# Writing own-column rows from a resident tile instead of gathering them, and leaving W times a to the general path

## The chip, the cores and the metric

The kernel runs on one core of one Trainium2 chip. The metric is the device time of one execution in microseconds. Each run of the kernel executes the whole program once; three runs of the kernel before gave 234.99 to 235.19 us, median 235.16.

## The reference

A graph attention layer with four heads, followed by a residual sum and a layer norm, all in float32, N = 4096 nodes with D = 512 features:

```python
ht = (h @ W).reshape(N, 4, 512).transpose(1, 0, 2)
src = einsum('hnd,hd->hn', ht, a_src); dst = einsum('hnd,hd->hn', ht, a_dst)
e = leaky_relu(src[:, :, None] + dst[:, None, :], 0.01) + adj[None]
att = softmax(e, axis=-1)
out = layernorm(x + einsum('hij,hjd->hid', att, ht).mean(axis=0))
```

`adj` (4096 x 4096) holds zeros and, at the edges and on the whole diagonal, values drawn uniformly from 0.05 to 1e9. It is added to the scores inside the softmax. Where the largest value of a row exceeds the second by more than the scores can differ, the softmax is one at that column and zero elsewhere, for all heads alike. Then row i of the output is layernorm(x[i] + x[col(i)] @ mean of the heads of W), with col(i) the column of the row's largest value.

## The kernel before

`leading_rows` computes that short form for all rows, and a test proves for each row that it is exact. The test compares the gap between a row's two largest values with a bound on the scores: the largest norm of a row of x times the largest sum of two norms of W times a. `general`, the full computation, stands behind a branch that is taken only where the test fails for some row.

The 4096 rows are cut into 32 blocks of 128. Block ib takes rows p*32 + ib, one for each partition p. For each block:

- `load_adj` loads the adjacency tile adj_t, 128 x 4096, 2 MB, on the SP queue. Six buffers; in iteration t the tile of block t+5 is issued, which waits until VectorE has read the tile of block t-1.
- `segment_maxima` (line 180, VectorE) reduces each row to the maxima of segments of 16 values (32 from block 18 on, 64 for the last four).
- `find_segment` (lines 187, 189, VectorE) finds the largest segment, and `fetch_segment` (lines 196, 200, POOL) fetches that segment of each row from memory by an indirect DMA into the tile lead.
- `find_column` (lines 217, 223, VectorE; 225, POOL) finds the place within the segment, adds the segment's start on POOL, and `gather_rows` (line 211, POOL) fetches row col of x for each of the 128 rows by an indirect DMA into the tile y, 256 KB a block. y has four buffers.
- `turn` (line 238 TensorE, 240 ScalarE) transposes y into yt; `residual` (line 246) puts x's own rows, resident in the tile hold, into the PSUM tile o by a product with the identity; `products` (line 253) adds yt times w_sum, the mean of W's heads.
- `stats` (lines 275, 277, ScalarE) sums o and its squares, `row_norm` (line 260, ScalarE) sums the squares of x's row for the bound, `rstd` (lines 280 to 282, POOL) makes the factor of the layer norm, `finish` (line 286, ScalarE) writes the result into hold, and stores follow after the loop.

hold is one tile for all 32 blocks. Its upper half holds W at first, 16 pieces of 128 x 512; x's blocks from 16 on are loaded over it once W is used.

W times a is computed in iterations 1 to 14, one or two pieces an iteration: `turn_w` transposes a piece (line 359 TensorE, 361 ScalarE), and `head_vector` multiplies it with the transposed a (line 367). `head_norms` makes the norms in iteration 16.

The order on every engine is the order in which the program emits the instructions (`tc.manual_schedule()`); each engine runs its queue in that order. The main loop runs t from 0 to 31 and emits, in this order: the loads of SP; the first half of block t's segment maxima; find_column of block t-2 with its gather; the second half; rstd for a pair of blocks (even t); find_segment of block t with its fetch; the transposes of W; turn, residual and products of block t-3; stats and row_norm of block t-4; the two finishes of the pair. Blocks 24 to 31 leave this pattern: blocks 24 to 27 are put by without the residual, and blocks 28 to 31 are finished after the loop.

Of the kernel before, what the change touches and what calls it, by code (L numbers as in the profile page):

```python
# [26 lines left out]
LAST = 4  # L27


@with_exitstack  # L30
def gat_resnorm_kernel(
    ctx: ExitStack,
    tc: tile.TileContext,
    x: bass.AP,
    adj: bass.AP,
    W: bass.AP,
    a: bass.AP,
    out: bass.AP,
):
# [19 lines left out]
    v = keep.tile([P, KB, 2 * H], F32, name="v")  # L59
    n_bad = keep.tile([1, NB], I32, name="n_bad")  # L60
    any_bad = keep.tile([1, 1], I32, name="any_bad")

    leading_rows(tc, x, adj, W, a, out, ident, v, n_bad, any_bad)

    flag = nc.values_load(any_bad[0:1, 0:1], min_val=0, max_val=N)
    with tc.If(flag > 0, preferred_fallthrough_block=True, label="general"):
        general(tc, x, adj, W, out, ident, v, n_bad)
# [3 lines left out]
def leading_rows(ctx, tc, x, adj, W, a, out, ident, v, n_bad, any_bad):  # L71
# [11 lines left out]
    KB, NB = D // P, N // P  # L83
    AHEAD = 5
# [5 lines left out]
    once = ctx.enter_context(tc.tile_pool(name="once", bufs=1))  # L90
# [3 lines left out]
    LEADS = (8, 8, LAST)  # L94
    small = ctx.enter_context(tc.tile_pool(name="small", bufs=5))
# [6 lines left out]
    x_rows = x.rearrange("(p nb) d -> p nb d", nb=NB)  # L102
    out_rows = out.rearrange("(p nb) d -> p nb d", nb=NB)
# [3 lines left out]
    once.tile([P, 24], F32, name="pad")  # L107
    hold = once.tile([P, NB, D], F32, name="hold")
    w_at = NB - KB * H
    w_sum = once.tile([P, KB, D], F32, name="w_sum")  # L110
    a_rows = once.tile([2 * H, D], F32, name="a_rows")

    once.tile([P, 32], F32, name="pad_end")
# [5 lines left out]
    def load_adj(ib):  # L119
        if 0 <= ib < NB:  # L120
            t = adj_t[ib] = adj_pool.tile([P, N], F32, name="adj_t")
            n = pieces(ib)
            for k in range(n):
                nc.sync.dma_start(t[:, ts(k, N // n)], adj_rows[ib][:, ts(k, N // n)])  # L124

    def load_x(lo, n):
        nc.sync.dma_start(hold[:, ds(lo, n), :], x_rows[:, ds(lo, n), :])
# [19 lines left out]
    for e, lo, hi in spans:  # L147
        nc.gpsimd.iota(
            first[:, lo:hi], pattern=[[N // e, hi - lo]], base=lo * N // e, channel_multiplier=NB * N // e
# [10 lines left out]

# [47 lines left out]

    def gather_rows(ib, col):
        y = y_t[ib] = y_pool.tile([P, D], F32, name="y")  # L210
        nc.gpsimd.indirect_dma_start(  # L211
            out=y, out_offset=None, in_=x,
            in_offset=bass.IndirectOffsetOnAxis(ap=col[:, :1], axis=0),
        )

# [18 lines left out]
    def turn(ib):  # L234
        y = y_t.pop(ib)
# [3 lines left out]
        yt = yt_of[ib] = rows.tile([P, KB, P], F32, name="yt")  # L239
        nc.scalar.copy(yt, tp)  # L240

# [95 lines left out]
    def store(queue, lo, n):  # L337
        queue.dma_start(out_rows[:, ds(lo, n), :], hold[:, ds(lo, n), :])
# [7 lines left out]
    at_d = once.tile([P, KB, 2 * H], F32, name="at_d")  # L346
    vn = once.tile([P, 1], F32, name="vn")
    pv = psum.tile([P, KB, 2 * H], F32, name="pv", bufs=1)

    def turn_a():  # L350
        tp = psum.tile([P, KB, P], F32, name="tp", bufs=2)
        for k in range(KB):
            nc.tensor.transpose(tp[:, k, : 2 * H], a_rows[:, ts(k, P)], ident[: 2 * H, : 2 * H])
        nc.scalar.copy(at_d, tp[:, :, : 2 * H])

    def turn_w(kb, h):
        tp = psum.tile([P, KB, P], F32, name="tp", bufs=2)
        for k in range(KB):
            nc.tensor.transpose(tp[:, k, :], hold[:, w_at + kb * H + h, ts(k, P)], ident)  # L359
        wt = rows.tile([P, KB, P], F32, name="wt")  # L360
        nc.scalar.copy(wt, tp)  # L361
        return wt

    def head_vector(kb, h, wt):

        for k in range(KB):
            nc.tensor.matmul(  # L367
                pv[:, kb, h : 2 * H : H], wt[:, k, :], at_d[:, k, h : 2 * H : H],
                start=(k == 0), stop=(k == KB - 1),
            )  # L370

    def head_norms():
        nc.vector.tensor_copy(v, pv)
        vv = once.tile([P, KB, 2 * H], F32, name="vv")
        nc.vector.tensor_mul(vv, v, v)
        pn = psum.tile([P, KB, 2 * H], F32, name="px", bufs=1)
        nc.tensor.matmul(pn, ones, vv, start=True, stop=True)
        n2 = once.tile([P, 2 * H], F32, name="n2")
        nc.vector.tensor_reduce(n2, pn.rearrange("p k c -> p c k"), axis=AX.X, op=OP.add)
# [47 lines left out]
    x_at = {Q - 1: (Q, 2 * Q), 3 * Q - 1: (3 * Q, Q), 4 * Q - 1: (4 * Q, 2 * Q)}  # L427
    vectors = [(kb, h) for kb in range(KB) for h in range(H)]
    vectors_at = {t: 2 if t < 3 else 1 for t in range(1, 15)}
    COLUMN, PROJECT, STATS, FINISH = 2, 3, 4, 6  # L430

    for t in range(NB):
# [12 lines left out]
        pair = FINISH <= t < BEHIND + FINISH and t % 2 == 0  # L445
# [11 lines left out]
        if t == 0:  # L457
            turn_a()
        turned = [(*vectors[0], turn_w(*vectors.pop(0))) for _ in range(vectors_at.get(t, 0))]
# [97 lines left out]
def general(ctx, tc, x, adj, W, out, ident, v, n_bad):  # L557
# [10 lines left out]
    H = v.shape[2] // 2  # L568
# [9 lines left out]
    with ExitStack() as pre:  # L578
        sd_all = pre.enter_context(tc.tile_pool(name="all", bufs=1)).tile([2 * H, N], F32, name="sd_all")
# [4 lines left out]
        for kb in range(KB):  # L584
            nc.gpsimd.dma_start(w_sb[:, kb, :], w_blocks[:, kb, :])
        for g in range(NCH):
            xT = two.tile([P, KB, C], F32, name="xT")
            for q in range(Q):
                ps = pps.tile([P, KB, P], F32, name="ps_x")
                for kb in range(KB):  # L590
                    nc.tensor.transpose(ps[:, kb, :], x_sb[:, g * Q + q, ds(kb, P, KB)], ident)
# [11 lines left out]
        for g in range(NCH):  # L603
            pt = pps.tile([P, Q, 2 * H], F32, name="ps_s")
            for q in range(Q):
                rows_of = sd_all[:, ds(g * Q + q, P, NB)]
                nc.tensor.transpose(pt[:, q, :], rows_of, ident[: 2 * H, : 2 * H])
            nc.vector.tensor_copy(src[:, ts(g, Q), :], pt[:, :, :H])
# [6 lines left out]
    def block(ib):  # L615
        src_i = stat.tile([P, H], F32, name="src_i", bufs=1)
        nc.vector.tensor_copy(src_i, src[:, ds(ib, 1), :].rearrange("p o h -> p (o h)"))
        held = psum.tile([P, D], F32, name="o_ps", bufs=1)
        adj_t = score.tile([P, N], F32, name="adj_g")
        nc.gpsimd.dma_start(adj_t, adj[ds(ib, P, NB), :])  # L620
# [39 lines left out]
        nc.gpsimd.dma_start(r, x[ds(ib, P, NB), :])  # L660
# [10 lines left out]
        nc.gpsimd.dma_start(out[ds(ib, P, NB), :], r)  # L671

    with tc.For_i(0, NB, 1) as ib:
        of_block = stat.tile([1, 1], I32, name="of_block", bufs=1)
        nc.vector.tensor_copy(of_block, n_bad[0:1, ds(ib, 1)])
        here = nc.values_load(of_block[0:1, 0:1], min_val=0, max_val=P)
        with tc.If(here > 0):
            block(ib)
# [28 lines left out]
```

## Time and profile before

| what | value |
|---|---|
| median of three runs | 235.16 us |
| span of the profiled execution, first to last instruction | 233.4 us |
| VectorE busy | 191.3 us (82%) |
| TensorE matmuls busy | 199.9 us (86%) |
| ScalarE busy | 111.8 us (48%) |
| POOL busy | 100.7 us (43%) |
| bytes moved by DMA | 97.12 MB |
| mean granted TensorE clock | 0.965 |

The times of the trace count from the start of the span. The runs' times hold in addition what lies before the first and after the last instruction; the median is 1.8 us above the span. The profiled execution has no other time of its own than its span. In a line of a group or timeline, the text behind the length is engine, line, operation, the tile written and the tiles read, and in brackets the idle time before it and what ended it.

### The profile page before, as it was taken

What the parts mean: (1) busy time and instruction counts of PE and PEld (TensorE: products, weight loads), DVE (VectorE), ACT (ScalarE), POOL (GpSimd) and SP (SyncE); (2) the same over time, 40 slices, a digit from 0 to 9 for tenths busy, and PEclk for the clock granted to TensorE, in tenths of its full rate; (3) what the DMA queues carried; (4) which work ended last, traced back from release to release, by engine and by line L of the source; (5) the groups of instructions that cost most, each with busy time, mean ns of one, the idle gap of its engine ahead of it and who ended that gap; (6) DMA issues with size and microseconds to landing.
All of it is one profiled execution on the core that took longest, in us unless ns stands there. A gap on an engine that the chain in (4) does not pass through costs nothing.

```text
span 233.4 us, 2484 instructions
## 1 busy us (share of the span) xinstructions
PE 199.9 (86%) x683; PEld 105.3 (45%) x683; DVE 191.3 (82%) x300; ACT 111.8 (48%) x267; POOL 100.7 (43%) x215
## 2 busy tenths in 40 slices
PE   0069995999999999999999779879998977999980
PEld 0034644646565555665645244334443433444460
DVE  0548299689929999999788995999999999998881
ACT  2001223014474757575767455545664644188561
POOL 2020234414524464644543452647464564548300
PEclk9999999579999999999999979999999999999997
DMA  6999999999999999999999999999999999999995
GB/s 237 423 432 428 428 438 426 415 439 436 422 421 437 423 431 425 431 419 428 430 430 428 432 423 432 423 430 421 426 433 420 426 423 426 412 424 420 421 414 213
DMA packets 12257, 97.12 MB, mean 416 GB/s; under 512 B 1992, under 2 KB 2440, under 8 KB 6480
## 3 DMA queue, kind: packets, MB, share of 16 engines
q1 hardware_dynamic: 8640, 88.08, 89.1%
q0 software_dynamic: 3584, 8.84, 9.6%
q8 instruction: 6, 0.10, 0.2%
q14 instruction: 11, 0.09, 0.1%
q10 hardware_dynamic: 16, 0.02, 0.0%
HBM read 88.54 MB, written 8.39 MB: 415 GB/s over the span
## 4 chain that ended last, share of the span: by engine, by line
DMA 64%; DVE 21%; PE 11%; SPq 1%; issue 1%; ACT 0%; DVEq 0%
DMA adj_t<-in_adj_dram 53%; DVE seg L180 17%; DMA hold<-in_x_dram 11%; PE o L253 6%; PE o L295 2%; DVE at L189 1%; PE tp L238 1%; DVE top L187 1%; PE o L246 1%; DVE within L223 1%; SPq L130 1%; PE o L291 0%; SPq L124 0%; DVE inner L217 0%; ACT hold L335 0%
## 5 line engine op out<-in xcount | busy, mean ns | idle before, releaser
L180 DVE TENSOR_REDUCE seg<-adj_t 128x128 f32<-128x2048 f32 (+3 forms) x66 | 145.5, 2208 | 28.5 <-DMA adj_t<-in_adj_dram 28.2
L253 PE MATMUL o<-w_sum,yt 128*128 128x512 f32 x248 | 117.6, 616 | 0.7 <-ACT yt L240 0.7
L253 PEld LDWEIGHTS o<-w_sum,yt 128*128 128x128 f32 x248 | 45.6, 196 | 55.2 <-issue 43.9
L240 ACT COPY yt<-tp 128x512 f32<-128x512 f32 x32 | 18.8, 588 | 43.9 <-PE tp L238 43.8
L200 POOL DMA_INDIRECT lead<-in_adj_dram,row x32 | 32.3, 1008 | 14.6 <-POOL row L196 14.6
L211 POOL DMA_INDIRECT y<-in_x_dram,col x32 | 30.9, 964 | 15.4 <-POOL col L225 15.1
L238 PE MATMUL tp<-ident,y 128*128 128x128 f32 x128 | 22.1, 296 | 10.2 <-DMA y<-in_x_dram,col 10.1
L246 PE MATMUL o<-hold,ident 128*128 128x512 f32 x52 | 28.5, 634 | 1.7 <-DMA hold<-in_x_dram 1.7
L343 PE MATMUL o<-hold,ident 128*128 128x512 f32 x32 | 17.3, 696 | 13.6 <-DMA hold<-in_L_gnn_W_dram 13.6
L238 PEld LDWEIGHTS tp<-ident,y 128*128 128x128 f32 x128 | 18.5, 209 | 22.8 <-issue 20.5
L361 ACT COPY wt<-tp 128x512 f32<-128x512 f32 x16 | 9.2, 587 | 38.2 <-PE tp L359 38.2
L196 POOL TENSOR_TENSOR row<-at,first 128x1 uint32<-128x1 uint32 x32 | 6.1, 190 | 43.6 <-DVE at L189 43.6
L367 PEld LDWEIGHTS pv<-at_d,wt 128*128 128x128 f32 x128 | 17.2, 200 | 7.4 <-ACT wt L361 3.7
L260 ACT ACTIVATE sq<-hold 128x512 f32<-128x512 f32 x32 | 19.8, 620 | 0.0
L225 POOL TENSOR_TENSOR col<-start,within 128x1 uint32<-128x1 uint32 x31 | 5.9, 190 | 32.2 <-DVE within L223 32.2
L286 ACT ACTIVATE hold<-o,nm,sd 128x512 f32<-128x512 f32 x24 | 17.2, 771 | 0.0
L277 ACT ACTIVATE sq<-o,nm 128x512 f32<-128x512 f32 x24 | 16.5, 687 | 0.8
L343 PEld LDWEIGHTS o<-hold,ident 128*128 128x128 f32 x32 | 6.9, 225 | 21.5 <-issue 21.5
L367 PE MATMUL pv<-at_d,wt 128*128 128x2 f32 x128 | 16.0, 249 | 0.6 <-ACT wt L361 0.6
L344 ACT ACTIVATE w_sum<-o 128x512 f32<-128x512 f32 x4 | 2.4, 598 | 27.5 <-PE o L343 27.5
L275 ACT ACTIVATE sq<-o 128x512 f32<-128x512 f32 x24 | 14.5, 606 | 0.0
L187 DVE MAX8 top<-seg 128x8 f32<-128x256 f32 (+2 forms) x32 | 11.6, 362 | 1.1
(86 smaller groups left out, 140.0 us busy)
## 6 DMA issues: line engine op xcount, KB each, us to landing
adj_t<-in_adj_dram SPq DMA_DIRECT2D x28, 2048.0 KB, 30.8
adj_t<-in_adj_dram SPq DMA_DIRECT2D x6, 1024.0 KB, 28.1
hold<-in_L_gnn_W_dram SPq DMA_DIRECT2D x2, 2048.0 KB, 16.4
hold<-in_x_dram SPq DMA_DIRECT2D x2, 2048.0 KB, 37.6
out_dram<-hold SPq DMA_DIRECT2D x4, 1024.0 KB, 16.1
out_dram<-hold SPq DMA_DIRECT2D x7, 512.0 KB, 14.4
hold<-in_x_dram SPq DMA_DIRECT2D x3, 1024.0 KB
adj_t<-in_adj_dram SPq DMA_DIRECT2D x4, 512.0 KB, 19.8
```

The source lines that it names most:

```text
L180: nc.vector.tensor_reduce(seg_of[ib][:, ts(k, N // e // n)], adj_t[ib][:, ts(k, N // n)].rearrange("p (s e) -> p s e", e=e), axis=AX.X, op ...
L200: nc.gpsimd.indirect_dma_start(out=lead, out_offset=None, in_=adj_segs[e], in_offset=bass.IndirectOffsetOnAxis(ap=row[:, :1], axis=0),)
L211: nc.gpsimd.indirect_dma_start(out=y, out_offset=None, in_=x, in_offset=bass.IndirectOffsetOnAxis(ap=col[:, :1], axis=0),)
L238: nc.tensor.transpose(tp[:, kb, :], y[:, ds(kb, P, KB)], ident)
L240: nc.scalar.copy(yt, tp)
L246: nc.tensor.matmul(o_ps[ib], ident, hold[:, ib, :], start=start, stop=False)
L253: nc.tensor.matmul(o_ps[ib], yt_of[ib][:, kb, :], w_sum[:, kb, :], start=(start and kb == 0), stop=(kb == KB - 1),)
L260: nc.scalar.activation(sq, hold[:, ib, :], AF.Square, accum_out=xx[:, ib : ib + 1])
L277: nc.scalar.activation(sq, o, AF.Square, bias=nm[:, i], accum_out=sd[:, i])
L286: nc.scalar.activation(hold[:, ib, :], o_ps.pop(ib), AF.Identity, bias=nm[:, i], scale=sd[:, i])
L343: nc.tensor.matmul(o, ident, hold[:, w_at + kb * H + h, :], start=(h == 0), stop=(h == H - 1))
L367: nc.tensor.matmul(pv[:, kb, h : 2 * H : H], wt[:, k, :], at_d[:, k, h : 2 * H : H], start=(k == 0), stop=(k == KB - 1),)
```

## The change

Five things are done together.

- In blocks 4 to 23, POOL compares each row's column with the row's own number. ScalarE writes y from hold, x's own rows, scaled by the comparison (one or zero). POOL adds 8192 to the index where the column is the row's own, which puts it beyond the bound of 4095, and the gather skips such rows. The gather writes the other rows of y over the zeros, so it follows ScalarE's write.
- The x loads of blocks 4 to 23 are issued two iterations earlier, since hold is now read one iteration earlier; x's block 0 is loaded by itself.
- The blocks are cut differently: block 0 is rows 0 to 127, and block ib from 1 on takes rows 128 + p*31 + ib - 1.
- The test's bound uses the Frobenius norm of W's heads times the norm of a instead of the norm of W times a. 16 square sums of W's pieces (iterations 3 to 14) and one of a replace the transposes and products; W times a is computed in the general path alone.
- finish runs seven instead of six iterations behind, in odd iterations; PSUM's o has five buffers instead of four, in the place of the tile pv.

```diff
+SKIP = 8192
+OWN = range(4, 24)
...
-    psum = ctx.enter_context(tc.tile_pool(name="psum", bufs=4, space=bass.MemoryType.PSUM))
-    adj_rows = adj.rearrange("(p nb) m -> nb p m", nb=NB)
+    psum = ctx.enter_context(tc.tile_pool(name="psum", bufs=5, space=bass.MemoryType.PSUM))
+    adj_rows = adj[P:, :].rearrange("(p nb) m -> nb p m", nb=RB)
...
     def load_x(lo, n):
-        nc.sync.dma_start(hold[:, ds(lo, n), :], x_rows[:, ds(lo, n), :])
+        if lo == 0:
+            nc.sync.dma_start(hold[:, 0, :], x[:P, :])
+            lo, n = 1, n - 1
+        if n:
+            nc.sync.dma_start(hold[:, ds(lo, n), :], x_rows[:, ds(lo - 1, n), :])
...
+    load_x(0, 1)
     for ib in range(KB // 2 + 1, AHEAD):
         load_adj(ib)
-    load_x(0, Q)
+    load_x(1, Q - 1)
...
+    numbers = once.tile([P, NB], I32, name="numbers")
+    nc.gpsimd.iota(numbers, pattern=[[1, NB]], base=P - 1, channel_multiplier=RB)
+    own = once.tile([P, NB], F32, name="own")
+    nc.gpsimd.tensor_copy(own, numbers)
...
+    def skipped(ib, col):
+        away = None
+        if ib in OWN:
+            y = y_t[ib] = y_pool.tile([P, D], F32, name="y")
+            same = small.tile([P, 1], F32, name="same")
+            nc.gpsimd.tensor_scalar(same, col, own[:, ib : ib + 1], None, op0=OP.is_equal)
+            nc.scalar.activation(y, hold[:, ib, :], AF.Copy, scale=same)
+            away = small.tile([P, 1], U32, name="away")
+            nc.gpsimd.tensor_scalar(away, same, float(SKIP), None, op0=OP.mult)
+        return away
+
     def gather_rows(ib, col):
-        y = y_t[ib] = y_pool.tile([P, D], F32, name="y")
+        if ib not in OWN:
+            y = y_t[ib] = y_pool.tile([P, D], F32, name="y")
+            nc.gpsimd.indirect_dma_start(
+                out=y, out_offset=None, in_=x,
+                in_offset=bass.IndirectOffsetOnAxis(ap=col[:, :1], axis=0),
+            )
+            return
+        there = small.tile([P, 1], U32, name="there")
+        nc.gpsimd.tensor_tensor(there, col, skipped(ib, col), op=OP.add)
         nc.gpsimd.indirect_dma_start(
-            out=y, out_offset=None, in_=x,
-            in_offset=bass.IndirectOffsetOnAxis(ap=col[:, :1], axis=0),
+            out=y_t[ib], out_offset=None, in_=x,
+            in_offset=bass.IndirectOffsetOnAxis(ap=there[:, :1], axis=0),
+            bounds_check=N - 1, oob_is_err=False,
         )
...
+    def square_sum_of_w(k):
+        sq = rows.tile([P, D], F32, name="sq")
+        nc.scalar.activation(sq, hold[:, w_at + k, :], AF.Square, accum_out=ww[:, k : k + 1])
...
-    x_at = {Q - 1: (Q, 2 * Q), 3 * Q - 1: (3 * Q, Q), 4 * Q - 1: (4 * Q, 2 * Q)}
-    vectors = [(kb, h) for kb in range(KB) for h in range(H)]
-    vectors_at = {t: 2 if t < 3 else 1 for t in range(1, 15)}
-    COLUMN, PROJECT, STATS, FINISH = 2, 3, 4, 6
+    x_at = {1: (Q, 2 * Q), 3 * Q - 3: (3 * Q, Q), 4 * Q - 3: (4 * Q, 2 * Q)}
+    squares = list(range(KB * H))
+    squares_at = {t: 2 if t < 7 else 1 for t in range(3, 15)}
+    COLUMN, PROJECT, STATS, FINISH = 2, 3, 4, 7
...
-        for some in turned:
-            head_vector(*some)
-        if ib >= 0:
             products(ib, 0, KB if ib < BEHIND else KB - 1)
+        for _ in range(squares_at.get(t, 0)):
+            square_sum_of_w(squares.pop(0))
```

More of the change, by code (lines that the diff above doesn't have):

```diff
@@ L364, in head_vector @@
[L364 to L370, printed above, removed]
-    def head_norms():
[L373 to L377, printed above, removed]
+    ww = once.tile([P, KB * H], F32, name="ww")
@@ L457, in leading_rows @@
         if t == 0:
-            turn_a()
-        turned = [(*vectors[0], turn_w(*vectors.pop(0))) for _ in range(vectors_at.get(t, 0))]
+            square_sums_of_a()
         if t == 16:
@@ L556, in general @@
 @with_exitstack
-def general(ctx, tc, x, adj, W, out, ident, v, n_bad):
+def general(ctx, tc, x, adj, W, a, out, ident, n_bad):
     nc = tc.nc
@@ L602, in general @@
                 nc.vector.tensor_copy(dst_b[:, h, ts(g, C)], pb)
[L603 to L608, printed above, removed]
+        for ib in range(NB):
+            pt = pps.tile([P, 2 * H], F32, name="ps_s")
+            rows_of = sd_all[:, ds(P + ib - 1, P, RB)] if ib else sd_all[:, :P]
+            nc.tensor.transpose(pt, rows_of, ident[: 2 * H, : 2 * H])
+            nc.vector.tensor_copy(src[:, ib, :], pt[:, :H])
     score = ctx.enter_context(tc.tile_pool(name="score", bufs=1))
```

124 lines of the change are left out of this document (80 added, 44 removed).

## The prediction

> **What bounds the kernel now.** I read the page's header and queues first, then the busy time in stretches, then the waits.
>
> ```profile
> span 233.4 us, 2484 instructions
> DMA  6999999999999999999999999999999999999995
> GB/s 237 423 432 428 428 438 426 415 439 436 422 421 437 423 431 425 431 419 428 430 430 428 432 423 432 423 430 421 426 433 420 426 423 426 412 424 420 421 414 213
> DMA packets 12257, 97.12 MB, mean 416 GB/s; under 512 B 1992, under 2 KB 2440, under 8 KB 6480
> q1 hardware_dynamic: 8640, 88.08, 89.1%
> q0 software_dynamic: 3584, 8.84, 9.6%
> ```
> ```profile
> 53.30:114.90 61.60, 61.60 (x263) 36.95 (x263) 55.45 (x81) 36.47 (x91) 31.14 (x66) 1.00 1.01 427
> 114.90:176.20 61.30, 54.69 (x150) 24.61 (x148) 54.64 (x85) 35.70 (x86) 30.77 (x64) 0.97 1.01 429
> ```
> ```profile
> DVE seg L180 <- DMA adj_t<-in_adj_dram: 28.2, 11, 8.7
> ```
>
> The 16 DMA engines are full from the second slice to the last but one. Between 53.3 and 176.2 us (the columns behind the length are PE, PEld, DVE, ACT, POOL, clock, DMA share, GB/s) the DMA share is 1.01 at 427 to 429 GB/s; VectorE is busy 55.45 of 61.60 us, ScalarE 36.47. VectorE waits for adjacency tiles, 28.2 us in all. So the transfers set the pace, VectorE stands close behind, and ScalarE, POOL and TensorE have room **as throughput**. The change must be judged by latency too, so next come the landings and one block's period.
>
> ```profile
> adj_t<-in_adj_dram SPq DMA_DIRECT2D x28, 2048.0 KB, 30.8
> lead<-in_adj_dram,row POOLq DMA_INDIRECT x32, 6.1
> y<-in_x_dram,col POOLq DMA_INDIRECT x32, 7.8
> DMA to landing us min/median/max: 6.2/7.8/9.5
> ```
> ```profile
> 53.31 2.27 DVE L180 TENSOR_REDUCE seg<-adj_t 128x128 f32<-128x2048 f32 x1
> ...
> 80.49 2.27 DVE L180 TENSOR_REDUCE seg<-adj_t 128x128 f32<-128x2048 f32 x1
> ...
> 86.15 2.27 DVE L180 TENSOR_REDUCE seg<-adj_t 128x128 f32<-128x2048 f32 x1
> ...
> 142.66 2.29 DVE L180 TENSOR_REDUCE seg<-adj_t 128x64 f32<-128x2048 f32 x1 [2.37 <-DMA adj_t<-in_adj_dram]
> 144.86 0.18 DVE L217 MAX8 inner<-lead 128x8 f32<-128x32 f32 x1
> ...
> 176.25 2.29 DVE L180 TENSOR_REDUCE seg<-adj_t 128x64 f32<-128x2048 f32 x1
> ```
>
> The fourth line is the spread of the row gathers of line 211. Iterations 6, 10, 11, 20 and 26 of the main loop start on VectorE at 53.31, 80.49, 86.15, 142.66 and 176.25. Undisturbed, VectorE needs 86.15 - 80.49 = 5.66 us a block. Iterations 6 to 25, in which the changed blocks 4 to 23 get their rows, take 176.25 - 53.31 = 122.9 us, or 6.15 us each, two x loads among them. An adjacency tile lands 30.8 us after its issue: the SP queue holds some five blocks of work, so VectorE may fall many us behind before the DMA engines run dry.
>
> **What the change removes.** Counted on the reference's own inputs, 205 of the 2560 rows of blocks 4 to 23 have their largest adjacency value on the diagonal. Their 205 x 2 KB = 0.42 MB are 1.0 us at 416 GB/s, if a skipped descriptor costs nothing; 0 if it costs what a fetched one does. The second part takes work off TensorE:
>
> ```profile
> L359 PE MATMUL tp<-ident,hold 128*128 128x128 f32 x64 | 9.3, 273 | 0.0
> L367 PE MATMUL pv<-at_d,wt 128*128 128x2 f32 x128 | 16.0, 249 | 0.6 <-ACT wt L361 0.6
> L361 ACT COPY wt<-tp 128x512 f32<-128x512 f32 x16 | 9.2, 587 | 38.2 <-PE tp L359 38.2
> ```
>
> That is 9.3 + 16.0 = 25 us of TensorE in iterations 1 to 14. On ScalarE 16 copies of 0.59 become 17 square sums of the kind of line 260 (below): 0.61 start to start, so nothing is saved there. TensorE does not set the pace, so the 25 us are worth nothing directly. In return the bound becomes looser; on the inputs the smallest gap between a row's two largest values is 10880, against a bound that rises from about 180 to about 1670, so the general path stays unused.
>
> **What it adds on POOL and ScalarE.** Per block there are three POOL instructions (compare, multiply, add) ahead of the gather, and one ScalarE copy that writes the gather's destination y; so the gather must wait for that copy. These rows of iterations 20 and 21 price it:
>
> ```profile
> 146.02 0.97 POOL L211 DMA_INDIRECT y<-in_x_dram,col  x1 [0.54 <-POOL col L225]
> 147.06 0.19 POOL L280 TENSOR_SCALAR sd<-sd 128x2 f32<-128x2 f32 x1
> 147.34 0.72 POOL L281 TENSOR_TENSOR sd<-sd,power 128x2 f32<-128x2 f32 x1
> 147.79 0.72 PE L238 MATMUL tp<-ident,y 128*128 128x128 f32 x4 [0.99 <-DMA y<-in_x_dram,col]
> 148.29 0.19 POOL L196 TENSOR_TENSOR row<-at,first 128x1 uint32<-128x1 uint32 x1
> 148.55 0.59 ACT L240 COPY yt<-tp 128x512 f32<-128x512 f32 x1 [3.49 <-PE tp L238]
> 148.98 1.07 POOL L200 DMA_INDIRECT lead<-in_adj_dram,row  x1 [0.50 <-POOL row L196]
> 149.03 0.60 ACT L275 ACTIVATE sq<-o 128x512 f32<-128x512 f32 x1
> 149.76 0.69 ACT L277 ACTIVATE sq<-o,nm 128x512 f32<-128x512 f32 x1
> 150.44 0.62 ACT L260 ACTIVATE sq<-hold 128x512 f32<-128x512 f32 x1
> 151.05 1.44 ACT L286 ACTIVATE hold<-o,nm,sd 128x512 f32<-128x512 f32 x2
> ...
> 154.62 0.72 PE L238 MATMUL tp<-ident,y 128*128 128x128 f32 x4 [1.73 <-DMA y<-in_x_dram,col]
> ```
>
> A small POOL operation that uses the one before starts 147.34 - 147.06 = 0.28 us after it: three are 0.8 us a block. POOL is busy 31 of 61 us, so as throughput that is covered by its idle time; without the cover it would be 20 x 0.8 = 16 us.
>
> The copy itself is unpriced. The nearest rows, one 128x512 pass, run from 0.59 (L240) to 0.72 (half of the L286 pair); I take 0.62, the row that reads the same tile (L260). **What matters is its place.** In iteration t it is emitted for block t-2 ahead of that iteration's own ScalarE work, so it stands behind all of iteration t-1's: the copy of block t-4's transposed rows (L240), squares, stats (L275, L277), row norm (L260) and, in odd t-1, the pair of finishes (L286). But L240 for block t-4 needs the rows of block t-4's gather. So the gather of block b can't start before the gather of b-2 has landed and been turned. Before, no such tie existed: the gather waited only for POOL's column.
>
> For even b the tie costs, from one gather's start to that of two blocks on: landing 7.8; from TensorE's transposes to the end of the finishes 151.05 + 1.44 - 147.79 = 4.70; the new copy 0.62; **13.1 us**. Where a square sum stands between (iterations 7, 9, 11, 13) it is 0.61 more, by the start-to-start of L260 to L286: 13.7. VectorE does two blocks in 11.3. The finishes move by one iteration (7 instead of 6 behind), which only chooses which parity has them.
>
> **The rule that speaks on this price.** The Trainium skill, page "DMA: Bandwidth & Descriptors", section "Anatomy of one DMA — SWDGE (gpsimd) path", fits such a transfer by 2.0 us and its bytes at 436 GB/s; 256 KB would take an estimated 2.6 us. By that the tie would be 2.6 + 4.70 + 0.62 = 7.9 us and hidden. The trace's 7.8 us, with full queues, decides.
>
> **How it adds up.** The x load of blocks 4 to 11 now goes ahead of adjacency tile 6 instead of tile 8: 2.1 MB at 427 GB/s, so iteration 6 starts 4.9 us later, at 58.2; tile 8 comes as before. Its gather started 146.02 - 142.66 = 3.36 after its iteration; with 0.8 for POOL, block 4's starts at 62.4. Nine steps lead to block 22's: 4 x 13.7 + 5 x 13.1 = 120.3, so 182.7. The next victim is VectorE: POOL fetches block 24's segment (row, lead) behind the gather it waits in: 0.97 + 0.19 + 0.51 + 6.1 = 7.8, so it lands at 190.5. VectorE needs it 144.86 - 142.66 = 2.2 us into iteration 26, which thus starts at 188.3 in place of 176.25: **12.0 us late**. That it is late by less than the sum of the steps' excess is because a gather may trail its column by some 5 us before a segment comes late.
>
> From block 24 on nothing is coupled, and VectorE, full there, can't catch up. Something comes back in the tail, since loads and most stores are done by then:
>
> ```profile
> 202.84 1.22 DVE L180 TENSOR_REDUCE seg<-adj_t 128x16 f32<-128x1024 f32 x1 [0.16 <-DMA adj_t<-in_adj_dram]
> 204.23 0.09 DVE L223 MATCH_VALUE_LOAD within<-top,lead 128x8 f32 x1 [0.17 <-DMA lead<-in_adj_dram,row]
> ...
> 207.19 1.22 DVE L180 TENSOR_REDUCE seg<-adj_t 128x16 f32<-128x1024 f32 x1 [0.23 <-DMA adj_t<-in_adj_dram]
> ```
> ```profile
> 214.56 0.96 POOL L211 DMA_INDIRECT y<-in_x_dram,col  x1 [0.30 <-issue]
> ...
> 221.63 0.72 PE L238 MATMUL tp<-ident,y 128*128 128x128 f32 x4
> ```
> ```profile
> out_dram<-hold SPq DMA_DIRECT2D x2, 256.0 KB, 4.3
> ```
>
> The waits of the last block, 0.16 + 0.17 + 0.23 = 0.6, go. The last gather takes 221.63 - 214.56 = 7.1 until TensorE has it; on emptier queues between 7.1 and the 4.3 of a store of the same size, and the last store gains something as well. I take 3.4 in all for both (bounds 0 and 4). Sum: 12.0 - 0.6 - 3.4 = +8.0 on the span of 233.4, 241.4. The runs' median of 235.16 lies 1.8 above that span, so the forecast is **243.2 us**. The 1.0 us of saved bytes is not in it: in this case the engines wait.
>
> Everything else I cost at nothing. Four short POOL operations at the start are covered: POOL idles there until the first segment is found. The early x load of block 0 (0.26 MB, 0.6 us) delays tile 3, for which VectorE is late anyway. The norms in iteration 16 wait for one product of TensorE, now later with the rest: 0 to 2 us, inside the same lag.
>
> Its own range comes from the landing: nine steps at 7.0 instead of 7.8 take 7.2 off, at 8.5 add 6.3; with the tail's bounds 237 to 250.
>
> **The rivals.**
> 1. *The tie is hidden and the bytes count*: 235.2 - 1.0 = **234.2**. It decides where 13.1 falls to 11.3, so a landing near 6.0. For it: the lowest row gather is 6.2, VectorE is 5.66 against a DMA pace of 6.15, and the TensorE work that goes away stood in front of the transposes. Against: the median is 7.8, and it is contention with queues that stay full.
> 2. *The tie costs just its slack*: at landings near 6.3 VectorE comes a few tenths late and the 1.0 us pays for it: **235.2**.
> 3. *Faster loads*: adjacency rows of one tile lie 31 instead of 32 rows of 16 KB apart. If everything ran at the best slice's 439 GB/s, 149 us of full stages at 427 would shrink by 2.7%, 4 us, and with rival 1 the time is **230**. Against: 427 is within 3% of the best slice already, and transfers don't matter while the tie holds. The same skill page, section "Latency and other measured facts", reports 207 GB/s at a pitch of 512 KiB against 214 padded, per direction; that is 3.4%, which no run here shows.
> 4. *A skipped descriptor is fetched all the same*: rival 1 ends at **235.2**; the forecast does not change.
>
> **Chances.** The forecast 0.74 (slower); rival 1 0.15 and rival 3 0.04 (faster, 0.19); rivals 2 and 4 0.07 (same). About 0.2%, 0.5 us, is what a measurement of this kernel can tell from no change. The forecast's own range of 237 to 250 holds too little alone, so the range reaches to rival 1: 233.8 to 250.
>
> **What would show it.** Right: POOL's row gather waits for ScalarE's new copy in most of blocks 4 to 23; gathers of even blocks start 13 to 14 us apart; VectorE waits for lead at the maxima of line 217 by 10 us or more in all, and for adjacency tiles hardly at all after iteration 12; the DMA share falls in the last fifth. The skipping shows as q0's bytes falling by 0.4 MB. Wrong: a DMA share still at 1.0 throughout, VectorE's waits still for adj_t, landings near 6 us; then the time is rival 1's.

## The result, and the profile after

The changed kernel takes **256.34 us** (median of 4 runs, 254.92 to 257.19) against 235.18 us (4 runs, 234.99 to 235.29) for the kernel before: a ratio of 1.0895 with a 95% interval of 1.0861 to 1.0929. Medians and ratios use the runs within 1.5% of a kernel's fastest; one run of experiment 3, at 259.75 us, lies beyond. The profiled execution took 256.06 us, 254.5 of them in the span: 21.1 us more span than before, where +8.0 was forecast. The sign was right; the time lies 13 us above the forecast and 6 above the range.

The page's header and queues of the changed kernel:

```profile
span 254.5 us, 2248 instructions
DMA  7999999999999999999999999989999999983134
GB/s 248 421 440 426 426 431 425 432 433 421 437 421 439 421 420 434 434 426 431 431 431 426 430 432 417 404 344 396 376 373 396 386 381 418 424 296 89 43 144 194
q0 software_dynamic: 3584, 8.42, 8.8%
```

Its DMA view (KB of one issue, median us from issue to landing):

```profile
adj_t<-in_adj_dram SPq DMA_DIRECT2D x28, 2048.0 KB, 23.7
lead<-in_adj_dram,row POOLq DMA_INDIRECT x32, 6.4
y<-in_x_dram,there POOLq DMA_INDIRECT x20, 8.3
```

The skipping works: q0 moved 8.42 MB instead of 8.84, the 0.42 MB that were counted. But from slice 25 to 35 the rate is 344 to 424 GB/s, and in the last four slices 43 to 194, because the loads have run out while the rest of the kernel is still behind. The time from an adjacency tile's issue on the SP queue to its landing fell from 30.8 to 23.7 us in the median: VectorE frees buffers so late that the queue drains.

The busy time in stretches (length, then PE, PEld, DVE, ACT and POOL busy, clock, DMA share, GB/s):

```profile
53.30:114.90 61.60, 42.00 (x105) 18.89 (x103) 46.93 (x65) 34.24 (x87) 29.77 (x72) 0.92 1.01 428
114.90:176.20 61.30, 46.39 (x122) 21.41 (x122) 45.77 (x74) 34.11 (x80) 32.84 (x82) 0.92 0.99 416
176.20:202.80 26.60, 21.55 (x58) 9.57 (x58) 22.27 (x32) 16.32 (x40) 16.97 (x42) 0.96 0.97 383
202.80:254.50 51.70, 45.03 (x140) 22.62 (x138) 43.43 (x90) 30.68 (x74) 24.08 (x43) 0.96 0.66 251
```

Between 53.3 and 176.2 us TensorE, VectorE and ScalarE are all *less* busy than before: VectorE has 46.93 and 45.77 us where it had 55.45 and 54.64, ScalarE 34.24 and 34.11 where it had 36.47 and 35.70 (TensorE has also lost the work on W times a). Nothing became a throughput bound. Something waits; the waits say what (us in total, times, longest):

```profile
POOL y L245 <- ACT y L230: 29.8, 16, 4.3
DVE seg L194 <- DMA adj_t<-in_adj_dram: 24.2, 5, 8.9
DVE inner L251 <- DMA lead<-in_adj_dram,row: 23.4, 13, 4.2
POOL y L245 <- PE px L403: 3.7, 1, 3.7
DVE w L406 <- PE px L404: 1.9, 1, 1.9
```

POOL's gather (L245) waits for ScalarE's copy (L230) in most of the twenty blocks, and VectorE waits 23.4 us for lead, where it hardly waited before. The wait put down to TensorE's px is a false name: px had nothing to do with that gather, which started at 139.47, 0.80 us after the end of ScalarE's copy (137.96 + 0.71 in the timeline); the two ended close together. So it is with the three gathers whose waits the view puts down to other work: each of the twenty starts 0.77 to 0.80 us after the end of its own copy.

One turn of the loop, from the gather of block 8 to that of block 10, in the chain of waits (start, us, what; "issue" is time without a wait that the profile shows); the first line is block 4's gather:

```profile
62.53 8.79 DMA y<-in_x_dram,there
...
93.77 8.17 DMA y<-in_x_dram,there
101.94 0.14 issue
102.07 1.11 PE tp L271 x4
103.21 0.59 ACT yt L273
103.80 0.62 ACT sq L392 x2
104.42 0.59 ACT sq L312 x2
105.03 0.03 ACT sq L314
105.06 0.55 issue
105.61 0.19 ACT sq L314
105.80 0.61 ACT sq L297 x2
106.41 1.34 ACT hold L323 x2
107.75 0.62 ACT y L230
108.37 0.03 POOLq L245
108.40 0.56 issue
108.98 0.16 issue
109.14 8.39 DMA y<-in_x_dram,there
```

This is the tie of the prediction, link by link: landing, transposes, ScalarE's queue in its order (transposed rows, W's square sum, stats, row norm, the two finishes), the copy, the next gather. It takes 15.37 us for two blocks, and VectorE undisturbed needs 11.3. From block 17 on the chain goes by the odd blocks (gathers at 173.18, 185.87 and 198.04), which have the same tie without the finishes.

### The profile page after: what moved, and what is told of

Same layout as the page of the kernel before. It is cut to its first block, busy times and chain, and to the rows that moved or that the text cites. A ratio compares the mean times of both kernels' runs of the same rounds, so it can differ in the third digit from the quotient of the medians.

```text
span 254.5 us, 2248 instructions
## 1 busy us (share of the span) xinstructions
PE 186.0 (73%) x489; PEld 86.3 (34%) x489; DVE 191.5 (75%) x301; ACT 126.8 (50%) x304; POOL 117.4 (46%) x278
## 3 DMA queue, kind: packets, MB, share of 16 engines
q0 software_dynamic: 3584, 8.42, 8.8%
HBM read 88.54 MB, written 8.39 MB: 381 GB/s over the span
## 4 chain that ended last, share of the span: by engine, by line
DMA 51%; PE 20%; ACT 12%; issue 7%; POOL 4%; DVE 3%; SPq 0%; POOLq 0%
DMA y<-in_x_dram,there 26%; DMA adj_t<-in_adj_dram 20%; PE o L290 12%; PE tp L271 4%; DMA y<-in_x_dram,col 3%; DVE seg L194 3%; ACT hold L323 3%; ACT y L230 2%; DMA lead<-in_adj_dram,row 2%; PE o L283 2%; ACT sq L297 2%; ACT sq L312 2%; ACT yt L273 2%; PE o L332 1%; ACT sq L392 1%
## 5 line engine op out<-in xcount | busy, mean ns | idle before, releaser
L290 PE MATMUL o<-w_sum,yt 128*128 128x512 f32 x248 | 119.5, 624 | 3.4 <-ACT yt L273 3.4
L290 PEld LDWEIGHTS o<-w_sum,yt 128*128 128x128 f32 x248 | 48.0, 203 | 69.5 <-issue 47.8
L273 ACT COPY yt<-tp 128x512 f32<-128x512 f32 x32 | 18.7, 584 | 84.1 <-PE tp L271 83.9
L271 PE MATMUL tp<-ident,y 128*128 128x128 f32 x128 | 23.9, 314 | 45.6 <-DMA y<-in_x_dram,there 34.9
L245 POOL DMA_INDIRECT y<-in_x_dram,there x20 | 22.1, 1105 | 43.2 <-ACT y L230 29.8
L271 PEld LDWEIGHTS tp<-ident,y 128*128 128x128 f32 x128 | 19.5, 209 | 65.5 <-issue 56.1
L214 POOL DMA_INDIRECT lead<-in_adj_dram,row x32 | 32.2, 1008 | 11.6 <-POOL row L210 11.6
L283 PE MATMUL o<-hold,ident 128*128 128x512 f32 x52 | 32.4, 713 | 0.0
L383 PE MATMUL o<-hold,ident 128*128 128x512 f32 x32 | 16.9, 695 | 13.8 <-DMA hold<-in_L_gnn_W_dram 13.8
L251 DVE MAX8 inner<-lead 128x8 f32<-128x16 f32 (+2 forms) x32 | 5.2, 182 | 23.4 <-DMA lead<-in_adj_dram,row 23.4
L230 ACT ACTIVATE y<-hold,same 128x512 f32<-128x512 f32 x20 | 14.3, 717 | 8.6 <-POOL same L229 8.6
L238 POOL DMA_INDIRECT y<-in_x_dram,col x12 | 11.6, 964 | 5.2 <-POOL col L259 4.0
L201 DVE MAX8 top<-seg 128x8 f32<-128x256 f32 (+2 forms) x32 | 11.6, 361 | 1.1
## 6 DMA issues: line engine op xcount, KB each, us to landing
adj_t<-in_adj_dram SPq DMA_DIRECT2D x28, 2048.0 KB, 23.7
```

Of the source, the lines that this page charges most:

```text
L214: nc.gpsimd.indirect_dma_start(out=lead, out_offset=None, in_=adj_segs[e], in_offset=bass.IndirectOffsetOnAxis(ap=row[:, :1], axis=0),)
L230: nc.scalar.activation(y, hold[:, ib, :], AF.Copy, scale=same)
L245: nc.gpsimd.indirect_dma_start(out=y_t[ib], out_offset=None, in_=x, in_offset=bass.IndirectOffsetOnAxis(ap=there[:, :1], axis=0), bounds_c ...
L271: nc.tensor.transpose(tp[:, kb, :], y[:, ds(kb, P, KB)], ident)
L283: nc.tensor.matmul(o_ps[ib], ident, hold[:, ib, :], start=start, stop=False)
L290: nc.tensor.matmul(o_ps[ib], yt_of[ib][:, kb, :], w_sum[:, kb, :], start=(start and kb == 0), stop=(kb == KB - 1),)
```

## The experiments

The edits of 1 to 7 are made to the changed kernel, the later ones to the kernel that each names. Ratios are to the kernel before, with 95% intervals.

**1. The new parts without own-column rows.** No block writes its own rows; the early x loads, W's square sums and the new cut of the blocks stay.

```diff
-OWN = range(4, 24)
+OWN = range(0)
```

> All of the change but the own-column part: no block is compared, copied or skipped; the new cut of the rows, the early x loads, the square sums and the later finishes stay. Theory (the tie between the row gathers of blocks b-2 and b through ScalarE's queue makes the loss): 234.5 to 236, all 21 us come back. Rival (the other parts of the change, above all the cut of the rows and the slower clock of a less busy TensorE, make a good part of it): above 240.

Measured: 235.92 us (235.82 to 236.31), ratio 1.0037 [1.0022, 1.0051]. All but 0.9 of the 21 us comes from blocks 4 to 23's own-column rows. The other parts together bring no gain, so the 25 us of TensorE work that went away bought nothing that shows, as the prediction said.

**2. The copy left out.** The gather waits for nothing of ScalarE. The kernel leaves the own rows unwritten, so its output differs.

```diff
-            nc.scalar.activation(y, hold[:, ib, :], AF.Copy, scale=same)
```

> ScalarE's copy into y is left out, so own rows of y hold what an earlier block left there; the three POOL operations and the skipping gather stay. Theory (tie): 233.8 to 235, the skipped 0.42 MB give about 1 us. Rival (POOL: three operations, and a checked gather of 1.105 us in place of 0.964, 20 times): stays above 245, since nothing of POOL's work is taken away. Rival (skipping itself slows the gather's landing): stays above 245.

Measured: 237.65 us (237.18 to 238.47), ratio 1.011 [1.0081, 1.0138]. One instruction of 0.72 us a block accounts for 18.7 of the 21 us. But the time lies 2.7 us above the expected range and 1.7 above experiment 1; the waits show where.

```profile
DVE inner L250 <- DMA lead<-in_adj_dram,row: 6.8, 11, 1.3
```

**3. Skipping left out.** Own rows are copied and then fetched all the same.

```diff
-SKIP = 8192
+SKIP = 0
```

> 0 in place of 8192 is added to the index, so every row is fetched, also the own ones; copy, comparison and bounds check stay. Theory (tie): 255 to 258, as the change; the bytes return and cost nothing, because the DMA engines are not what is waited for. Rival (skipping slows the landing): back to about 235. Rival (the bytes count even here): 1 us above the change.

Measured: 256.95 us (three runs, 255.68 to 257.08), ratio 1.0906 [1.087, 1.0943]. Against 1.0895 [1.0861, 1.0929] no difference can be told. The intervals reach some 0.8 us to each side, so the 1 us of the second rival isn't excluded; the first, that skipping slows the landing, is.

**4. The copy moved, not removed.** An unconditional copy of x's own rows into y, emitted at the top of an iteration for the block that is gathered in the next one.

```diff
+    def prefill(ib):
+        if ib in OWN:
+            y = y_t[ib] = y_pool.tile([P, D], F32, name="y")
+            nc.scalar.copy(y, hold[:, ib, :])
...
-            nc.scalar.activation(y, hold[:, ib, :], AF.Copy, scale=same)
...
+        prefill(t - 1)
         middle = 1 if t == NB - 1 else 2
```

> The copy into y is made of all rows, without the factor, and one iteration earlier in ScalarE's queue, since the gather overwrites all rows but the own ones; everything else as in the change, and the output is the same. The gather of block b then stands behind that of b-3, not b-2: about 15.2 us over three blocks, 5.1 a block, below VectorE's 5.66. Theory (tie): 234 to 236. Rival (POOL's operations): above 245. Rival (any write of ScalarE ahead of the gather costs, by the 0.77 us that POOL needs after it): about 240 or more.

Measured: 238.11 us (237.8 to 238.9), ratio 1.0137 [1.0114, 1.016]. ScalarE is busy 124.2 us against 126.8 in the changed kernel, and 18.2 us are gone. So what costs is the copy's **place** in ScalarE's queue, not the work that it adds to ScalarE. The time is 2.1 us above the expected range and 2.2 above experiment 1, much as in experiment 2, with VectorE waiting 6.9 us for lead.

**5. Own rows in the first half alone.**

```diff
-OWN = range(4, 24)
+OWN = range(4, 14)
```

> The own-column part for blocks 4 to 13 alone. Theory (tie): up to iteration 16 as in the change, where VectorE is 11.2 us behind the kernel without the part (127.6 against 116.4); from there it runs at its own 5.66 to 5.4 us a block and doesn't wait for the x loads of blocks 16 to 31, which gives some 5 back: 240 to 243. Rival (a loss in proportion to the blocks, 10 of 20): 246 or more.

Measured: 248.53 us (247.81 to 249.5), ratio 1.0569 [1.0533, 1.0605]. My expectation was 5.5 us or more too low; the rival's 246 or more came, though not in proportion to the blocks. VectorE's timeline at iterations 16 and 17 (start, us, instruction, in brackets the idle time before it):

```profile
127.44 2.27 DVE L194 TENSOR_REDUCE seg<-adj_t 128x128 f32<-128x2048 f32 x1
...
140.24 0.17 DVE L406 TENSOR_REDUCE w<-px 128x4 f32<-128x16 f32 x1 [2.72 <-PE px L404]
...
141.22 2.27 DVE L194 TENSOR_REDUCE seg<-adj_t 128x128 f32<-128x2048 f32 x1
...
216.61 1.20 DVE L194 TENSOR_REDUCE seg<-adj_t 128x16 f32<-128x1024 f32 x1
```

I had read the lag off at iteration 16's start, 127.44 - 115.8 = 11.6 us. The last tied gather and the norms then fall into iteration 16 itself, and iteration 17 starts 141.22 - 123.75 = 17.5 us late. From there VectorE caught up to 216.61 - 202.84 = 13.8 us at iteration 31: some 4 us in 14 iterations, because tiles were waiting for it. So the first ten blocks cost 14.0 us of span (247.4) and the last ten 7.1.

**6. The copy twice.**

```diff
             nc.scalar.activation(y, hold[:, ib, :], AF.Copy, scale=same)
+            nc.scalar.activation(y, hold[:, ib, :], AF.Copy, scale=same)
```

> ScalarE writes y twice, with the same values. Theory (tie): each of the nine steps from block 4's gather to block 22's grows by the copy's 0.62 to 0.72 us, 5.6 to 6.5 in all: 261 to 263. Rival (ScalarE has idle time, busy 127 of 254 us, so a copy more is free; the loss comes from POOL or from the landing alone): 256 to 257.

Measured: 262.63 us (262.03 to 263.34), ratio 1.1181 [1.1152, 1.1209], 6.3 us above the changed kernel. Nine steps of 0.62 to 0.72 are 5.6 to 6.5, as expected: what stands in the loop is paid once per step of two blocks, not once per block (twenty copies would be 12 to 14 us).

**7. No copy and no skipping.** Experiments 2 and 3 together.

> No copy into y, and 0 in place of 8192 added to the index: what stays of the own-column part is POOL's three operations and the bounds check. Theory (what was left over without the copy, 237.65 against 235.92, is POOL's longer queue, which fetches the segments late): 237.3 to 239, the skipped bytes being worth 0 to 1 us. Rival (the leftover comes from the skipping itself): 236.

Measured: 239.35 us (237.67 to 239.96), ratio 1.0166 [1.0121, 1.0212]. The leftover is not caused by the skipping. Against experiment 2 (1.011 [1.0081, 1.0138]) the intervals overlap: the bytes are worth between nothing and some 2 us once the tie is gone, which stays open.

**8. Less POOL work ahead of the segment fetch.** Experiment 4, with compare and multiply in one instruction, and the layer norm's factors (rstd) moved behind the fetch.

```diff
-            same = small.tile([P, 1], F32, name="same")
-            nc.gpsimd.tensor_scalar(same, col, own[:, ib : ib + 1], None, op0=OP.is_equal)
             away = small.tile([P, 1], U32, name="away")
-            nc.gpsimd.tensor_scalar(away, same, float(SKIP), None, op0=OP.mult)
+            nc.gpsimd.tensor_scalar(
+                away, col, own[:, ib : ib + 1], float(SKIP), op0=OP.is_equal, op1=OP.mult
+            )
...
-        if pair:
-            rstd(slice(t - FINISH, t - FINISH + 2))
...
         find_segment(t)
+        if pair:
+            rstd(slice(t - FINISH, t - FINISH + 2))
```

> The early copy of all rows, comparison and multiplication in one POOL operation (two on the way to the gather in place of three), and the three POOL operations of the layer norm's factor behind the segment's fetch instead of ahead of it. The output is the same. Theory (POOL's queue delays the segments): 0.3 us a block, and 1.3 more in odd iterations, come off the way to the segment's fetch, so VectorE no longer waits for lead: 234.3 to 236, and better than the run without the own-column part by the 1 us of bytes if nothing else is lost. Rival (the leftover is not POOL's): 237.5 to 238.2.

Measured: 237.85 us (237.03 to 237.94), ratio 1.0108 [1.0087, 1.013]: a miss. The waits:

```profile
DVE inner L254 <- DMA lead<-in_adj_dram,row: 5.4, 9, 1.9
```

The shorter way to the fetch gained nothing over experiment 4. Nor is it as short as planned: the rstd moved behind iteration 7's fetch (71.50 to 72.79) now stands right ahead of iteration 8's column, which POOL starts at 72.74, though VectorE had found its place by 72.11. The gather now starts 4.9 us after its iteration's start (iteration 8 at 69.4, gather of block 6 at 74.3; 3.36 in the prediction's rows), and the segment fetch of the same iteration is queued behind it.

**9. The gather behind the segment fetch.** Experiment 8, with the row gather issued after the iteration's segment fetch.

```diff
+        there = there_of[ib] = small.tile([P, 1], U32, name="there")
         nc.gpsimd.tensor_tensor(there, col, skipped(ib, col), op=OP.add)
+
+    def gather_late(ib):
+        if ib not in OWN:
+            return
+        there = there_of.pop(ib)
         nc.gpsimd.indirect_dma_start(
...
         find_segment(t)
+        gather_late(t - COLUMN)
```

> As the run with the early copy and the fused comparison, and the row gather of blocks 4 to 23 is issued behind the fetch of the next segments instead of ahead of it; the output is the same. Theory (what is left over, 237.85 against 235.92, comes from segments that land late because the row gather, 1.65 us later in its iteration, lies right ahead of them in POOL's queue and in the queue of its DMAs): VectorE's waits for lead go from 5.4 to under 1 us, and the time to 235 to 236.2. Rival (it comes from somewhere else): 237.5 to 238.2.

Measured: 235.81 us (235.47 to 236.53), ratio 1.0031 [1.0019, 1.0043]. The leftover is gone. Its waits have these lines for TensorE's product and for lead:

```profile
DVE w L415 <- PE px L413: 4.7, 1, 4.7
DVE within L266 <- DMA lead<-in_adj_dram,row: 1.0, 1, 1.0
```

At the other instruction that reads lead (L260 here, L254 in experiment 8) the wait fell from 5.4 to 0.2 us, and at this one from 1.3 to 1.0. So the own-column rows can be had for nothing measurable against experiment 1, and they bring nothing measurable either.

**10. Experiment 1 with the old cut.** Blocks take rows p*32 + ib again: pitch of 32 rows, block 0 not apart, one store fewer. Of the general path, which isn't entered, nothing is changed back.

```diff
-    adj_rows = adj[P:, :].rearrange("(p nb) m -> nb p m", nb=RB)
+    adj_rows = adj.rearrange("(p nb) m -> nb p m", nb=NB)
...
-            nc.sync.dma_start(hold[:, 0, :], x[:P, :])
...
-            queue.dma_start(out[:P, :], hold[:, 0, :])
```

> No own-column part, and the blocks cut as in the kernel before (rows p*32 + ib), with its loads of x's first blocks; early x loads, square sums and later finishes stay. The general path, which isn't entered, keeps the new cut. Theory (the 0.85 us of the run without the own-column part come from the new cut, through one more store in the tail and the last row gather behind it, 8.5 us in place of 6.9): 234.9 to 235.3. Rival (they come from the lighter TensorE or the x loads): 235.7 to 236.1. Rival of the row pitch (32 rows of 16 KB apart loads slower than 31): the loads take longer, 236.5 or more.

Measured: 235.41 us (235.19 to 236.01, 11 runs), ratio 1.0014 [1.0005, 1.0023], between the ranges of the theory and of its rival. By the ratios some 0.5 of experiment 1's 0.9 us goes with the new cut. It doesn't come by the way I expected: the last row gather still lands after 8.30 us with the old cut (8.39 with the new one, 6.9 in the kernel before), and only starts earlier, at 214.51 instead of 215.34. Loads are as fast at either pitch, as the stretches show, first with 31 rows (experiment 1), then with 32:

```profile
53.30:114.90 61.60, 50.28 (x133) 22.27 (x131) 54.02 (x77) 36.80 (x99) 29.48 (x61) 0.94 1.01 428
```
```profile
53.30:114.90 61.60, 51.83 (x137) 22.76 (x135) 54.21 (x77) 38.28 (x102) 29.33 (x61) 0.94 1.01 428
```

**11. Experiment 9 with the old cut.** The edits of 9 and 10 together.

> The run with the gather behind the segment's fetch, with the old cut of the blocks; the general path, which isn't entered, keeps the new cut. If both theories hold, the 1.0 us of skipped bytes is left over: 234.0 to 234.8, better than the kernel before. If the bytes are worth nothing, 235.0 to 235.4.

Measured: 237.45 us (237.12 to 238.5), ratio 1.0109 [1.0092, 1.0127], above both expected ranges, although the span was 233.3 to 234.6, within a microsecond of the 233.2 to 233.7 of the kernel before. 3.8 to 4.2 us of its time lie outside the span, 1.5 to 1.7 in the runs of the kernel before beside it, of the changed one and of experiment 9. Why isn't known, and no run here tells. The spans alone (median 233.5 against 233.6) show no gain from the skipped bytes either.

**12. The norms later.** Experiment 9, in which VectorE waits 4.7 us for TensorE's product of the norms in iteration 16.

```diff
-        if t == 16:
+        if t == 25:
             head_norms()
```

> The row gather behind the segment fetch, as in the experiment before, with the norms of W moved from iteration 16 to iteration 25. Theory: VectorE's one wait of 4.7 us for TensorE's product of the norms and the 12.0 us that iteration 16 took come from where the norms stand in VectorE's order; later the sums of squares are long done and TensorE's queue is shorter, so iteration 16 to 17 takes 7 to 8 us again, VectorE's wait for the product is under 2 us, and TensorE's backlog in the tail shrinks: 234.3 to 235.3 us. Rival: the wait only gives back what VectorE then waits for adjacency tiles, since the loads pace those stages: the time stays 235.5 to 236.2.

Measured: 240.15 us (239.72 to 240.96), ratio 1.0223 [1.0209, 1.0237]: a miss on the wrong side, 4.3 us slower than experiment 9. TensorE's timeline around the product:

```profile
174.40 0.72 PE L280 MATMUL tp<-ident,y 128*128 128x128 f32 x4
...
175.82 3.68 PE L299 MATMUL o<-w_sum,yt 128*128 128x512 f32 x8
179.34 0.29 PE L412 MATMUL px<-ww,ones 128*128 128x16 f32 x2
179.56 0.38 PE L413 MATMUL px<-each,ones 8*128 8x8 f32 x2
```
```profile
179.98 0.17 DVE L415 TENSOR_REDUCE w<-px 128x4 f32<-128x16 f32 x1 [4.91 <-PE px L413]
```

The two small products of the norms stand in TensorE's queue behind the transposes and products of the iteration before, at both places, and those need a gather's landing. Block 21's gather, at 166.31, lands after 8.0 us, and its transposes start at 174.40; since TensorE had worked without a pause from 154.81 on, its backlog and the landing aren't told apart there. In experiment 9, iteration 15, TensorE did wait for a landing (1.49 us, until 120.49). The gather there starts late in its iteration, in iteration 6 7.8 us after its start (65.3 against 57.5), so these products are late for VectorE. In iteration 16 that hid mostly under adjacency tiles that were late anyway: iteration 18 starts at 133.2, in experiment 1 at 132.0. By iteration 25 tiles lie ready, nothing hides it, and iteration 26 starts at 181.0 instead of 176.8.

None of these versions beats the kernel before.

## Why the prediction was wrong in size

| step of the prediction | predicted | measured |
|---|---|---|
| iteration 6 starts, later for the x load | 58.2 us | 57.8 |
| gather of block 4 starts | 62.4 us | 62.53 |
| nine steps of the tie, to block 22's gather | 120.3 us | 130.65 (193.18 - 62.53) |
| block 22's gather to block 24's segment in use | 7.8 us | 7.5 |
| lag of VectorE there | 12.0 us | 22.2 |
| given back in the tail | 4.0 us | 1.1 |
| sum on the span | +8.0 us | +21.1 |

The fourth and fifth lines come from POOL's and VectorE's timelines of the changed kernel: block 22's gather, iteration 26's start, and the use of lead in it, which the kernel before reached 2.2 us into the iteration, at 178.5. The landing of lead ended the wait, so it came at 200.7.

```profile
193.18 1.10 POOL L245 DMA_INDIRECT y<-in_x_dram,there  x1 [1.94 <-ACT y L230]
```
```profile
197.20 2.27 DVE L194 TENSOR_REDUCE seg<-adj_t 128x64 f32<-128x2048 f32 x1
200.78 0.09 DVE L257 MATCH_VALUE_LOAD within<-top,lead 128x8 f32 x1 [1.32 <-DMA lead<-in_adj_dram,row]
```

**The mechanism was right.** The tie through ScalarE's order is what the chain of waits walks; taking the copy out (2) or moving it (4) removes 18 to 19 us of the 21; doubling it (6) costs what nine steps cost. The prediction's signs came (gathers waiting for ScalarE, lead waits above 10 us, no wait for adjacency tiles after iteration 6, a falling DMA share in the last part, q0's 0.4 MB) but for the distance of even blocks' gathers: 15 to 16 us over the first five steps, then 14.4 falling to 12.2, instead of 13 to 14. Its rivals fell: the tie is not hidden (1, 2); no gain from the bytes shows (experiments 3 and 9); the pitch doesn't speed the loads (experiment 10); a skipped row is not fetched (q0).

**The failed step is the sum "landing 7.8 + 4.70 + 0.62 = 13.1 us", 13.7 with a square sum: above all the handoffs between engines, which it put at nothing.** By the chain of blocks 8 to 10 the turn is 15.37 us: landing 8.17 where I took 7.8; 0.13 until TensorE starts, taken as nothing; from the transposes to the end of the finishes 107.75 - 102.07 = 5.68 where 4.70 + 0.61 = 5.31 was taken; the copy 0.62 as taken; and 0.77 us from the copy's end to the start of POOL's gather, taken as nothing. Together 0.37 + 0.13 + 0.37 + 0.77 = 1.64 us in this step. The nine steps were, in order, 16.00, 15.24, 15.37, 15.20, 15.13, 14.37, 14.22, 12.88 and 12.24: above the forecast while the queues are full, below it at the end, when landings fall from 8.0 to 8.8 us (blocks 4 to 16, even) to 6.0 to 7.0 (18 to 22) while the load rate falls as well.

Over the nine steps the terms weigh differently from this one turn. The two handoffs are there each time, 0.13 to 0.14 and 0.77 to 0.80 us: some 8.2 us of the 10.4. The landings of the seven even blocks 4 to 16 lie 3.9 us in all above 7.8 each, and those of blocks 18 and 20 (6.7 and 6.0) 2.9 below: 1.0 together. The slower transposes came in three steps, the first, third and fifth: 1.1.

Two of these sizes stood in the trace before. *The landing* came from the median over all 32 gathers; from block 24 on these land in 6.2 to 7.5, and the mean over blocks 4 to 23 was 8.15 already. *The handoffs* between engines were left out at both ends of the sum, although the quoted row of the old gather shows 0.54 us of idling after POOL's own addition. *The transposes* were taken at 0.72 us, and in six of the nine steps they took that. In the other three they took 1.10, and there the granted clock was 0.50 (102.0 to 103.2 us, for one), where it was 1.00 beside a step of 0.72 (117.6 to 118.5). TensorE had idled about as long ahead of both, 3.40 and 4.38 us; what halves the clock is not shown here.

**A second, smaller failure is the tail**, "I take 3.4 in all for both". The landing's spread in the changed kernel:

```profile
DMA to landing us min/median/max: 3.4/8.1/10.1
```

The last gathers did land in 3.4 us, even below my bounds of 4.3 to 7.1 (that the saving I took is the same figure is chance). It didn't help, since they were no longer last. The chain's end:

```profile
207.79 8.18 DMA y<-in_x_dram,col
215.97 0.14 issue
216.10 0.72 PE tp L271 x4
...
243.93 0.47 PE tp L271 x4
```

The last landing on it is at 215.97; from then TensorE works off its backlog with hardly a pause until the output, and block 31's rows, gathered at 236.4 and landed by 239.8, are turned only at 243.93. Of the lag of 22.2 us at iteration 26, 1.1 came back. So the 13.1 us of error are 10.4 from the nine steps, 2.9 from the tail and -0.2 from the rest.

**The range** doesn't follow from its own terms. The landing's 7.2 down and 6.3 up with the tail's bounds give 243.2 - 7.2 - 0.6 = 235.4 to 243.2 + 6.3 + 3.4 = 252.9, not 237 to 250. The measured 256.34 lies outside either way, since no bound allowed for the handoffs.

**The rule of the page.** The Trainium skill's page "DMA: Bandwidth & Descriptors", section "Anatomy of one DMA — SWDGE (gpsimd) path", would give such a gather an estimated 2.6 us, by which the tie was hidden. The 3.4 us of the last gathers, with the loads over, come near it; the 8.0 to 8.8 us beside full queues don't, and these decided. The figures that rival 3 quotes from the same page of the Trainium skill are for copies between HBM tensors, and its 214 GB/s for a padded pitch of 4 MiB; the loads here ran at 428 GB/s at either pitch (experiments 1 and 10).

**What I had taken as covered.** The three POOL operations a block (0.8 us) were put down as hidden by POOL's idle time. With the tie they are; without it they, and the wider handoff, show as 1.7 to 2.2 us (experiments 2 and 4 against 1), by way of the segment fetch that stands behind the gather (8, 9). The norms in iteration 16 were "0 to 2 us, inside the same lag": VectorE's wait was 1.9, inside the bound. With later gathers it was longer: 4.7 in experiment 9 and 4.9 in experiment 12.

## What to carry to other kernels

Before an operation is put on an engine that has room, write down what stands ahead of it in that engine's queue and which landing that work waits for: if the new operation itself releases a transfer of the same stream, it closes a loop, and the loop's length against the period counts, not the engine's share of busy time. Size such a loop with the landings of that stage, with every handoff between engines as a term of its own, and with TensorE's durations at the clock that is granted there. If the copy is wanted, issue it early, where its input already lies ready, and let the fetch that is needed first go first in the queue.

## What the runs showed of the hardware beside that

- From ScalarE's copy to POOL's gather 0.77 to 0.80 us pass in all twenty blocks (108.37 to 109.14, for one); from POOL's own addition 0.54 before, and 0.63 on average in experiment 2. The gather that skips rows occupies POOL for 1.105 us, the plain one for 0.964.
- Rows that the bounds test leaves out move no bytes, though q0 lists 3584 packets either way.
- A small fetch queued closely behind a 256 KB gather on POOL's queue lands later. Between 62 and 130 us lead took 6.3 to 8.3 us in the changed kernel, median 7.8 (1.6 us behind the gather in even iterations, 3.0 in odd ones), and 5.9 to 7.9, median 6.1, in the kernel before, which mostly issues it 3.0 us or more behind (146.02 and 148.98 in the prediction's rows). With the fetch ahead of the gather (experiment 12) it took 6.0 to 6.8, median 6.3.
